# A two-layer Perceiver kernel: in the mixer's loop, the products with X one tile ahead of the next tile's B and C products, and each tile's norm one iteration later

## The chip, the core and the metric

The kernel runs on one core of a Trainium2 chip, in one launch. The metric is the device time of the launch in microseconds (us). Each engine of the core works through its own queue of instructions in order and waits on semaphores for the others: TensorE (PE: matrix products and transposes), VectorE (DVE: elementwise work and reductions), ScalarE (ACT: functions from a loaded table, and copies), GpSimd (POOL: elementwise work) and SyncE (SP: here it only issues DMAs).

## What is computed

Sixteen sequences of 64 tokens with 512 features pass through two layers, each of a cross attention, a mixer or self attention, and a feed-forward part, always as `x = x + f(layernorm(x))`. The change lies in the first layer's mixer, and what comes right behind it is the feed-forward part with a router:

```
x = x + _L0_attn_ref(_layernorm(x), ...)     # the mixer
x = x + _L0_ffn_ref(_layernorm(x), ...)      # 16 blocks, a router keeps 4 of them for each token

# mixer, for each of 16 heads
logA = einsum('hoc,bthc->btho', W_logA, x) + b_logA
XBC  = silu(einsum('hoc,bthc->btho', W_XBC, x) + b_XBC)      # X: 32, B: 64, C: 64 channels
cum  = cumsum(logA over t);  diff = cum[i] - cum[j]
A_ss = where(causal, exp(diff), 0)
G    = einsum('bihn,bjhn->bhij', C, B)
Y    = einsum('bhij,bjhc->bihc', A_ss * G, X)
gate = einsum('hoc,bthc->btho', W_gate, x) + b_gate
out  = (gate * Y).reshape(B, T, D) @ W_out.T + b_out
```

## The kernel before

The 1024 tokens lie as G = 8 tiles of 128 tokens (two sequences each). A tile's residual is `x[:, g, :]`, and `xnT` holds the normed tokens transposed, features on partitions, as the products want them. All data is 32-bit float, and every matrix product shows up as two records in the profile.

A norm is four steps: `ln_stats` (L114, two DVE instructions), `ln_scale` (L118, a square root on ACT and a reciprocal on DVE), `ln_norm` (L122, one DVE instruction that makes `xn`), and `ln_transpose` (L128, four PE transposes and an ACT copy into `xnT`). `ln_out` (L137) is the last two. ACT has one table of functions at a time. Square root, exponential and Silu are in different ones, and copies are in all of them, so each change from one to another costs a table load, which stands in ACT's queue.

The mixer is the stage at L527 to L673. First come the X channels and log A of all tiles (`make_x`), the gates (`make_gate`) and, for tiles 0 to 3, the B and C channels (`make_bc`: sixteen products into eight wide PSUM buffers, each emptied by two Silus). Then the loop over g has for each tile:

- `front(g)`: POOL makes `rt` (L608), PE sums it over time into `pd` (L612, two products), and ACT takes its exponential `ea` (L622). PE makes `pg`, the 32 products of B and C (L619). DVE masks `pg` into `mt` (L624) and multiplies `mt` by `ea` (L625).
- `back(g)`: PE makes `py`, the 32 products of X and `mt` (L637). DVE multiplies the gate by it (`gT`, L640). PE projects with `wout` (L643, four products), DVE adds that to `x` (L644).

The loop emits `front(g)` and then `back(g - 1)` and `ln_stats(g - 1)`. The square roots of tiles 0 to 3 are taken together at g == 4, those of 4 to 6 behind the loop. `ln_out` follows from g == 5 on with tiles 0 to 2, and tiles 3 to 6 behind the loop. At g == 4, `make_bc(1)` makes B and C of tiles 4 to 7. The last tile's `ln_out` stands in the feed-forward stage (L780).

What order the engines see isn't this one. The stage isn't pinned (only stage 1 uses `keep_in_program_order`), so a scheduler reorders each engine's queue when the kernel is built. In the built kernel before, PE's period is: `py(g-1)`, `pd(g+1)`, one product of `pg(g+1)`, the projection of g-1, [a transpose], the other 31 products of `pg(g+1)`.

PSUM is tight: `pw2` (L557) has three wide buffers of two banks for `pd`, `pg`, `py` and `pbc` in turn, and `ps2` (L556) two of one bank. `tmp` (L555) has two buffers of each of `rt`, `ea`, `mt`.

Behind the mixer stands the feed-forward stage (L686 on). Its `route(q)` (L721) needs `rwz`, a padded copy of the router's weights, which POOL makes (L702) from a DMA (L689). The route is a PE product `pr`, an ACT copy `lp`, PE's `pl`, seven DVE steps up to `rank`, and PE's transposes `pt` (L748). Its masks go to DRAM and come back by DMA (L750, L757), and DVE multiplies the hidden values by them (L773). In between, pieces of the last layer's weights are brought to their grid (`piece_load`, `piece_scale`, `piece_round`, `piece_store`, L156 to L176): a DMA in, three small DVE steps, one on POOL (L167), one on DVE (L171), one on POOL (L175), and a DMA out. Two of those pieces come right behind the mixer, in SBUF that `mt` used.

## Time and profile before

| | us |
|---|---|
| median of 3 runs | 2061.74 (2059.08 to 2063.44) |
| the profiled execution's own time | 2065.08 |
| its span, from first to last instruction | 2063.4 |
| PE busy in the span | 1957.7 (95%) |
| DVE, ACT, POOL busy | 1216.9, 804.8, 622.3 |
| mixer, from its first product to the router's first (1190.85 to 1299.26) | 108.4 |
| its loop, from the first `pg` (1216.95) to there | 82.3 |
| PE busy from 1217.0 to 1299.3 (19.96 + 18.20 + 22.87 + 11.15 in four stretches) | 72.2 |
| PE busy from 1312.0 to 1460.0 (32.91 + 55.00 + 60.00 in three stretches) | 147.9 of 148.0 |

The times of instructions count from the span's start. A row of the timeline is a run of equal instructions: start, duration, engine, line, operation, tile written and tiles read, shape, number of records, and in brackets how long the engine had been idle before it and what ended that. PE starts the next product before the last one's result is out, so work on PE is best measured from start to start[...]. The clock granted to PE was full in all stretches from 1190 to 1460.

### The profile page before, as it was taken

The numbers are of one execution on the slowest core, as the hardware profiler recorded it, in microseconds if no ns is written. First come the engines' busy times: TensorE is split into PE (matmuls) and PEld (weight loads), VectorE is DVE, ScalarE is ACT, GpSimd is POOL, SyncE is SP. The second block draws the span as 40 slices with busy tenths as digits, with TensorE's granted clock in tenths as the row PEclk, the third lists the DMA queues.
The fourth block names the chain that finished last, engine by engine and source line by source line (L and its number), as shares of the span: only waits on it lengthen the run. The fifth ranks groups of instructions, "written<-read, shape, count | busy, mean of one in ns | idle before, by whom it ended". The sixth has DMA issues, their size and how long they took to land. (4 is left out here: it accounts for less than half of the span.)

```text
span 2063.4 us, 39030 instructions
## 1 busy us (share of the span) xinstructions
PE 1957.7 (95%) x17197; PEld 1236.0 (60%) x17197; DVE 1216.9 (59%) x1869; ACT 804.8 (39%) x1112; POOL 622.3 (30%) x463
## 2 busy tenths in 40 slices
PE   8999999999999999999999798899998999999779
PEld 4677777777777677777777654444453455444334
DVE  2577777777777777777777654711113334429751
ACT  2445454545454544545454443201102123317700
POOL 0346454445445454635454321300003000000100
PEclk9999999999999999999999899999999999999889
DMA  5011101101110111011100120510236971200001
GB/s 207 22 54 44 45 20 54 44 24 42 51 46 17 48 44 54 12 54 44 54 12 17 32 103 22 197 50 31 84 131 247 347 278 62 71 0 10 21 0 41
DMA packets 61754, 141.13 MB, mean 68 GB/s; under 512 B 4448, under 2 KB 31600, under 8 KB 60432
## 3 DMA queue, kind: packets, MB, share of 16 engines
q1 hardware_dynamic: 61584, 138.63, 18.9%
q8 instruction: 135, 2.21, 0.5%
q14 instruction: 35, 0.29, 0.1%
HBM read 127.02 MB, written 11.60 MB: 67 GB/s over the span
## 5 line engine op out<-in xcount | busy, mean ns | idle before, releaser
L204 PE MATMUL ps<-wkv,ctxT 128*128 128x256 f32 (+1 forms) x1664 | 399.7, 388 | 16.5 <-DVE vt L229 16.3
L204 PE MATMUL ps<-ctxT,wkv 128*128 128x400 f32 (+1 forms) x1024 | 365.6, 503 | 12.7 <-DMA ctxT<-in_ctxT_dram 8.8
L204 PEld LDWEIGHTS ps<-wkv,ctxT 128*128 128x128 f32 (+1 forms) x1664 | 295.9, 185 | 96.2 <-DVE vt L229 26.8
L338 POOL TENSOR_TENSOR acc<-acc,st 128x1024 f32<-128x1024 f32 x124 | 319.6, 2577 | 23.0 <-ACT st L331 17.9
L265 ACT COPY st<-sc 128x1024 f32<-128x1024 f32 x192 | 191.7, 1016 | 320.5 <-PE sc L204 284.3
L229 DVE TENSOR_TENSOR vt<-ps,rows 128x256 f32<-128x256 f32 (+1 forms) x416 | 170.7, 421 | 202.0 <-PE ps L204 201.8
L204 PEld LDWEIGHTS ps<-ctxT,wkv 128*128 128x128 f32 x1024 | 189.7, 191 | 141.3 <-issue 12.8
L323 DVE TENSOR_TENSOR st<-st,nb 128x1024 f32<-128x1024 f32 (+1 forms) x224 | 239.1, 1139 | 34.3 <-PE nb L317 34.3
L218 ACT ACTIVATE kt<-ps,cols 128x400 f32<-128x400 f32 (+1 forms) x256 | 152.3, 595 | 271.2 <-PE ps L204 271.2
L331 ACT ACTIVATE st<-st 128x1024 f32<-128x1024 f32 (+1 forms) x224 | 212.1, 992 | 7.3 <-DVE st L323 6.9
L204 PEld LDWEIGHTS sc<-qd,kt 64*128 64x128 f32 x3072 | 179.2, 188 | 36.5 <-issue 24.2
L204 PE MATMUL sc<-qd,kt 64*128 64x128 f32 x3072 | 197.8, 278 | 1.6 <-ACT st L265 1.6
L336 POOL TENSOR_TENSOR acc<-st 128x1024 f32<-128x1024 f32 x31 | 73.0, 2356 | 353.3 <-issue 221.2
L280 DVE TENSOR_TENSOR rm<-rm,sc 128x512 f32<-128x512 f32 x256 | 168.5, 679 | 10.7 <-PE sc L204 3.8
L204 PE MATMUL av<-st,vt 128*32 128x64 f32 x6656 | 108.7, 223 | 8.8 <-DVE xnT L365 8.8
L59 PE MATMUL ps<-xnT,w 128*128 128x512 f32 x256 | 112.2, 594 | 0.0
L59 PE MATMUL ps<-w,hT 128*128 128x512 f32 x256 | 110.2, 592 | 0.0
L204 PEld LDWEIGHTS av<-st,vt 128*32 128x32 f32 x6656 | 98.5, 112 | 18.1 <-ACT st L331 9.1
L167 POOL TENSOR_TENSOR w<-w,winv 128x512 f32<-128x512 f32 x36 | 37.9, 1055 | 192.3 <-DVE winv L166 181.7
L59 PE MATMUL po<-wdT,gate 128*128 128x512 f32 x192 | 85.2, 607 | 3.2 <-DVE gate L1231 3.2
L1209 POOL TENSOR_TENSOR gate<-up,gate 128x1024 f32<-128x1024 f32 x4 | 9.5, 2385 | 259.0 <-ACT up L1208 259.0
L59 PEld LDWEIGHTS ps<-w,hT 128*128 128x128 f32 x256 | 48.6, 190 | 61.2 <-issue 61.2
(236 smaller groups left out, 2249.6 us busy)
## 6 DMA issues: line engine op xcount, KB each, us to landing
cT<-in_ctxT_dram SPq DMA_DIRECT2D x16, 1601.0 KB, 10.6
cN<-in_ctx_dram SPq DMA_DIRECT2D x16, 1536.0 KB, 9.7
ctxT<-in_ctxT_dram SPq DMA_DIRECT2D x15, 1601.0 KB, 7.3
grid<-w SPq DMA_DIRECT2D x36, 256.0 KB, 2.0
w<-grid SPq DMA_DIRECT2D x36, 256.0 KB, 2.7
w<-in_w_dram SPq DMA_DIRECT2D x2, 4096.0 KB
mk<-kept SPq DMA_DIRECT2D x16, 512.0 KB, 3.9
w<-in_wgate_dram SPq DMA_DIRECT2D x12, 256.0 KB, 2.6
```

The costliest lines, as they stand in the source:

```text
L59: pe.matmul(out, lhsT=lhsT, rhs=rhs, start=start, stop=stop)
L167: pin(gp.tensor_tensor(w, w, inv.unsqueeze(2).to_broadcast([P, 16, 32]), ALU.mult))
L204: pin(pe.matmul(out, lhsT=lhsT, rhs=rhs, start=start, stop=stop))
L218: pin(s.activation(kts[u, i][:, o:o + n], ps[:, :n], AF.Identity, bias=col(C_BK0 + c)))
L229: pin(v.tensor_tensor(t[:n, :], ps[:n, :], row(R_BV0 + e, 256)[:n, :], ALU.add))
L265: pin(s.copy(st[:, ks[0]:ks[-1] + 1, r * 256:(r + 1) * 256], sc[r]))
L280: pin(v.tensor_tensor(rm, rm, sc[r][:, z:z + 2, :], ALU.max))
L323: pin(v.tensor_tensor(f[:m, k:k + n, :], f[:m, k:k + n, :], nb[:m].unsqueeze(1).to_broadcast([m, n, 512]), ALU.add))
L331: pin(s.activation(f[:m, k:k + n, :], f[:m, k:k + n, :], AF.Exp))
L336: pin(gp.tensor_tensor(accs[u], f[:, 0:2, :], f[:, 2:4, :], ALU.add))
L338: pin(gp.tensor_tensor(accs[u], accs[u], f[:, k:k + 2, :], ALU.add))
L1209: gp.tensor_tensor(gate[:, f, :], up[:, f, :], gate[:, f, :], ALU.mult)
```

## The change

`front` is split into `decay(g)` (`rt` and `pd`) and `mixing(g, pd)` (`pg`, `ea`, `mt`), and `back` into `gated(g)` (`py`, `gT`) and `mixed(g)` (projection, addition to `x`, and now the norm's statistics, square root and reciprocal of this one tile). The loop emits `decay(g)`, `gated(g-1)`, `mixing(g)`, `mixed(g-1)`, `ln_out(g-2)`.

```
-            lah = la[:, g, :].rearrange("p (m r) -> p r m", r=2).unsqueeze(3).to_broadcast(shape)
...
-            return g, mt
-        def back(g, mt):
+            return mt
+        def gated(g, mt):
...
             v.tensor_tensor(gv, gv, pv, ALU.mult)
+        def mixed(g):
             po = ps2.tile([P, 512], F32, name="ps", tag="mm")
             for c in range(4):
                 mm(po, gT[:, c, g * P:(g + 1) * P], wout[:, c, :], c == 0, c == 3)
             v.tensor_tensor(x[:, g, :], x[:, g, :], po, ALU.add)
+            ln_stats(g)
+            ln_scale(g, g + 1)
...
-        pending = None
+        mt = None
         for g in range(G):
             if g == 4:
                 make_bc(1)
-            new = front(g)
-            if pending is not None:
-                back(*pending)
-                ln_stats(g - 1)
-                if g == 4:
-                    ln_scale(0, 4)
-                if g >= 5:
-                    ln_out(g - 5, ps2)
-            pending = new
-        ln_scale(4, 7)
-        back(*pending)
-        ln_stats(G - 1)
-        ln_scale(G - 1, G)
-        for g in range(3, G - 1):
-            ln_out(g, ps2)
+            pd = decay(g)
+            if g:
+                gated(g - 1, mt)
+            mt = mixing(g, pd)
+            if g:
+                mixed(g - 1)
+            if g >= 2:
+                ln_out(g - 2, ps2)
+        gated(G - 1, mt)
+        ln_out(G - 2, ps2)
+        mixed(G - 1)
```

What the scheduler makes of it, read from the built kernels, is this. No product, elementwise step or DMA is added or taken away except for the square roots and what belongs to them: eight square roots with eight reciprocals in place of three and three, and fifteen table loads in place of six from the first `ea` to the router.

- **PE** up to `pg(0)`: as before. Then in each iteration: `pd(g)`, `py(g-1)`, `pg(g)` in one piece, projection of g-1, transposes of g-2. The sixteen products of `make_bc(1)` stand in one piece behind the transposes of tile 1. The end is: ..., projection of 6, transposes of 5, `py(7)`, transposes of 6, projection of 7, three products of the feed-forward part, the router's `pr`. Before, it was `py(7)`, projection of 7, transposes of 3, 4, 5, 6, `pr`. Between `pr` and the transposes `pt` stand 9 products of the feed-forward part as before, so with the three ahead 12 are done by `pt`.
- **ACT** in each iteration: `ea(g)`, copy of the transposed tile g-2, table load, square root of g-1, table load, `ea(g+1)`.
- **DVE** in each iteration: both steps of `mt(g)`, addition to `x` of g-1, statistics of g-1, reciprocal, `xn` of g-1, `gT(g)`.
- **POOL**: the `rt` are as before, and the additions of the next bias to `x` (L143), each behind its tile's `xn`, stand between them; they stood behind all `rt`. Behind the mixer, both steps of both pieces now stand ahead of the making of `rwz`.
- **SP** behind the mixer: two piece loads, the store of the first piece, the load of the router's weights, the load of `w2` (4 MB). Before, the router's weights and `w2` stood ahead of that store.

More of the change, by code (lines that the diff above doesn't have):

```diff
@@ L599, in make_bc, with decay @@
                         s.activation(t_[:, pair, :], ps[:, r, :], AF.Silu, bias=col(b_ + pair))
-        def front(g):
-            BT, CT = bcs[g // 4]
-            shape = [P, 2, 8, LQ]
-            upto4 = upto.unsqueeze(1).unsqueeze(1).to_broadcast(shape)
+        shape = [P, 2, 8, LQ]
+        upto4 = upto.unsqueeze(1).unsqueeze(1).to_broadcast(shape)
+        def decay(g):
             lah = la[:, g, :].rearrange("p (m r) -> p r m", r=2).unsqueeze(3).to_broadcast(shape)
@@ L612, in front, with mixing @@
                 mm(pd[:, r, :], later, rt[:, r].rearrange("p m i -> p (m i)"))
+            return pd
+        def mixing(g, pd):
+            BT, CT = bcs[g // 4]
             pg = wide("pg")
```

## The prediction

> **What bounds the kernel now.** I read the page first: PE is busy for 1957.7 of 2063.4 us, so only time that PE loses can be won, and an edit that doesn't change PE's work is worth what it changes in PE's waits. Then I took the table of stretches. PE is busy for 147.9 of the 148.0 us from 1312.0 to 1460.0, behind the mixer, but for only 72.2 of the 82.3 us of the mixer's loop (front table). The list of PE's waits between 1210 and 1345 says for what:

> ```profile
> PE ps L59 <- DVE gT L640: 4.4, 7, 1.1
> PE py L59 <- DVE mt L625: 2.2, 1, 2.2
> PE pt L748 <- DVE rank L745: 2.0, 1, 2.0
> PE ps L131 <- DVE mv L116: 1.3, 1, 1.3
> PE ps L131 <- DVE xn L124: 0.9, 1, 0.9
> PE pd L59 <- ACT ea L622: 0.8, 1, 0.8
> PE ps L131 <- DVE x L644: 0.4, 1, 0.4
> ```

> These are 12.0 us in all: the projection waits for the gate in each iteration, the rest is at the loop's end and in the router. This is all that a new order can win. PE's timeline shows one period:

> ```profile
> 1267.33 3.70 PE L59 MATMUL ps<-wout,gT 128*128 128x512 f32 x8 [0.65 <-DVE gT L640]
> 1270.87 0.60 PE L131 MATMUL ps<-ident,xn 128*128 128x128 f32 x4
> 1271.39 1.16 PE L59 MATMUL pg<-CT,BT 64*64 64x64 f32 x62
> 1272.48 0.86 PE L59 MATMUL py<-mt,X 64*32 64x64 f32 x64
> 1273.27 1.98 PE L59 MATMUL pd<-rt,later 128*128 128x512 f32 x4
> 1275.18 0.32 PE L59 MATMUL pg<-CT,BT 64*64 64x64 f32 x2
> 1276.12 3.70 PE L59 MATMUL ps<-wout,gT 128*128 128x512 f32 x8 [0.62 <-DVE gT L640]
> ```

> From start to start: projection 3.54, transposes 0.52, pg 1.09, py 0.79, pd 1.91. That is 7.85 of work in a period of 8.79, so some 0.9 is lost in each.

> **The change, one period worked out.** S is the start of the projection of g-2. Without waits PE runs transposes at S+3.54, pd(g) at 4.06, py(g-1) at 5.97, pg(g) at 6.76, the next projection at 7.85. py no longer waits (mt(g-1) was ready a projection ago), and pg now lies between py and the projection as cover for gT (0.68). But gT has a new neighbour ahead of it in DVE's queue: the norm of g-2 with its own square root. That chain, with durations of the same timelines: projection's result S+3.70, x 0.72, statistics 0.73 and 0.18, so mv at S+5.37. ACT meanwhile copies the transposes (done S+4.82) and then loads the square root's table:

> ```profile
> 1266.51 1.28 ACT L622 ACT_TABLE_LOAD   x1 [1.87 <-PE pd L59]
> 1267.80 1.02 ACT L622 ACTIVATE ea<-pd 128x1024 f32<-128x1024 f32 x1
> ```

> 1.29 from load to next instruction: square root at S+6.12 to 6.42, reciprocal, xn from 6.66 to 7.2, gT to 7.9. The projection starts at S+7.9. So a period costs 7.9, with 0.05 of wait in place of 0.9. The second load (to the exponential) ends at S+7.7, ea(g) at 8.7, and mt's second step asks for it at 9.3: hidden, with 0.6 to spare.

> **Against it, first: the tables.** [...] The row shows no gap around the load, and I take it.

> **Against it, second: POOL.** rt(g+2) starts when pd(g) is out, S+6.04, and runs 1.91. What DVE's xn does beside POOL shows here (timeline, both engines, at the loop's end):

> ```profile
> 1294.97 1.04 POOL L167 TENSOR_TENSOR w<-w,winv 128x512 f32<-128x512 f32 x1
> 1295.12 1.56 DVE L124 TENSOR_SCALAR xn<-x,mv,rstd 128x512 f32<-128x512 f32 x1
> ...
> 1297.01 1.26 POOL L143 TENSOR_TENSOR x<-x,rows 128x512 f32<-128x512 f32 x1
> 1297.20 1.36 DVE L124 TENSOR_SCALAR xn<-x,mv,rstd 128x512 f32<-128x512 f32 x1
> ```

> xn takes 0.54 by itself, but 1.56 and 1.36 where it starts behind a POOL instruction: it sits until POOL is through. In the new period xn comes at S+6.66, half a us behind rt, so it is held to S+8.0, gT ends at 9.25, and the projection starts at S+9.2: 1.35 lost, more than before. That hits the iterations in which both stand together, xn of tiles 1 and 3 with rt of tiles 5 and 7 (xn of 0 has slack, xn of 2 falls into the B and C products, and from tile 4 on no rt is left). Bounds: 0 if xn gets in first, 2.7 for both. I take 2.7.

> **The loop's sum**, as starts of projections, from pg(0) at 1216.95, which nothing ahead moves. Tile 0: pd(1) and then py(0) waits 0.8 for the first mt: 1222.65. Tile 1 (no transposes): +7.37, 1230.0. Tile 2: +7.85 +1.35, 1239.2. Tile 3: the B and C products lie between. The first Silu comes at about 1246.9 (transposes, copy, two loads, one square root), each buffer is emptied in 1.14 (rows of L599), pd(4) may start when the sixth is, 1253.9, and pd, py, pg follow: 1257.7 (before: 1258.94, with one pd more behind it). Tiles 4, 5, 6: +9.2, +7.9, +7.9, 1282.8. At the end transposes of 5 and py(7) lead to 1287.7, and then the transposes of tile 6 stand ahead of the projection of 7 and need xn of 6, at S+7.2 = 1290.0: 2.4 of wait. Projection of 7 at 1290.5 (before: 1290.71), done at 1294.1. Before, four transposes and 2.6 of waits followed until the router at 1299.26; now they are behind us. So PE is 5.2 ahead.

> **What is given back behind it.** In SP's queue the load of the router's weights now stands behind the store of the first weight piece. That piece may be loaded when py(7) is done: 1287.75, landing 2.7 later (DMA issues) 1290.4. DVE's three steps (0.69, 0.17 held by POOL's L143, 0.24) end at 1292.3. POOL's two L167 take 1.05 each, 1294.45; DVE's L171 is held to there and both end at 1295.3; L175 1.05, 1296.35. Store issued, weights' load at 1296.8, landing 1299.5. POOL copies (L702, 0.44): rwz at 1300.0. PE does three products of the feed-forward part (2.6) to 1296.7 and then waits 3.3 for rwz. The router's pr starts at 1300.0 against 1299.26, but with 2.6 of work done ahead: 1.8 gained. Bounds of this wait: 2.3 to 4.3, by one POOL instruction's length either way.

> The wait for rank (2.0) goes: from pr to pt there are 9 products as before, but DVE is through with its norms, so lg comes right behind pl at 1302.9 (before 1304.0, and 0.8 of its steps lost to POOL) and rank at 1309.5, ahead of PE's 1310.15. The second router starts at 1314.0, before 1318.12: 4.1. There a new wait may come: rank of the second half goes between mask multiplies, the masks come by DMA 1.6 + 5.0 behind their store at 1311.7, so 1318.3 (before 1319.4), then DVE needs 9.6 to rank, 1327.9, and PE is there at 1327.1. 0.8 is given back: the second pt at 1328.1 against 1331.53, **3.4 us gained**. From there PE is dense in before, each mask multiply waiting for ACT and not for a mask, so I carry the gain to the end unchanged. w2 is issued 2.7 later (1297.2), takes some 12 (before: from 1294.5 until the DMA share falls off at 1306), and PE wants it at about 1358 (before 1362.0): hidden. The third piece load behind it, and the kept masks' store at 1311.7, come after w2 has drained.

> The profiled execution takes 2065.08, its span 2063.4; 3.4 less is 2061.7 and 2060.0. The median of the runs is 2061.74: **2058.3 us**.

> **Rivals.** (a) As worked out, 2056.5 to 2060: 0.45. (b) xn and rt don't collide, or the piece chain is shorter, so that rwz is early: 2.7 of collisions and 3.3 of wait are open, 6.0 in all; half of it gives 2055.3, all of it 2052.3. For it: the collision hangs on half a us; against it: xn waits for a table load that can't start before the copy. 0.25. (c) The gain moves into the router: the masks' store falls behind w2's 4 MB, which fills the queues for 12 us; each us of that delays the second rank and pt by one, and with 2 to 3 us nothing is left: 2061. The times say that w2 is drained at 1309; 0.2. (d) Slower: the switch of tables costs more than the row says, on the chain square root, xn, gT. [...] Against it: the rows. 0.1.

> **The numbers.** A measurement of this kernel tells 0.2%, 4.1 us, from no change: below 2057.6 is faster, above 2065.9 slower. (a) lies across the lower border, a quarter to a third of it below (0.13); (b) is below; (c) is no change; (d) is mostly above, with 0.02 of (c). Faster 0.38, same 0.52, slower 0.10. The range leaves out (d) and the far end of (b): 2054.5 to 2062.5.

> **What would show it.** Projections (L59 ps<-wout,gT) 7.9 apart without a wait for gT, but 9.2 for tiles 2 and 4, with xn of 1.3 or more in front; a load and the next ACT instruction 1.29 apart; PE's transposes of tile 6 waiting some 2.4 for xn; pr waiting some 3.3 for POOL's rwz; the second pt near 1328. If PE waits for gT in every period, (d) holds; if pr doesn't wait, (b).

## The result, and the profile after

The changed kernel takes 2055.54 us (median of 17 runs, 2050.64 to 2061.67), the kernel before 2062.47 (17 runs, 2059.08 to 2068.25); the ratio is 0.9965, 95% interval 0.9955 to 0.9974. That is some 7 us less (5.4 to 9.3 by the interval), where 3.4 were predicted. The profiled execution took 2056.32, its span 2054.6 (before 2065.08 and 2063.4).

A difference of two single spans says little here. In the fourteen profiles of this study, repeats of both kernels among them, the first `pg` of the loop starts anywhere between 1214.3 and 1217.5, though next to nothing ahead of it was touched. So I count from the first `pg`, and to the first product with `w2` (PE L59 ps<-w,hT), by which all of the router is over: 145.06 us before (1216.95 to 1362.01), 139.96 after (1215.15 to 1355.11). **5.1 us come from there.** The list of PE's waits, of 1210 to 1345 as before (line, what is waited for: us in total, times, longest):

```profile
PE ps L131 <- DVE xn L124: 2.3, 1, 2.3
PE ps L59 <- DVE gT L645: 2.2, 2, 1.1
PE pbc L59 <- ACT BT L599: 2.1, 1, 2.1
PE py L59 <- DVE mt L630: 0.8, 1, 0.8
PE pr L59 <- POOL rwz L709: 0.8, 1, 0.8
```

8.2 us in place of 12.0, and quite other ones: seven waits for gT have become two, those for rank and for the last mt are gone, and there is a new one of 2.1 in the B and C products, where ACT stands at a square root before its Silus. The list gives 3.8 of the 5.1. The rest is hidden in PE's busy time (132.85 before, 131.51 after, though the change runs 6.8 us of it at half clock, see below): a period before lost 0.94 from start to start where the list shows 0.65, since the profile's ends of products are modelled.

One period, PE's timeline, without the lines between (transposes, pd, py):

```profile
1265.14 3.70 PE L59 MATMUL ps<-wout,gT 128*128 128x512 f32 x8 [1.11 <-DVE gT L645]
...
1271.72 1.16 PE L59 MATMUL pg<-CT,BT 64*64 64x64 f32 x64
```

The next projection starts at 1272.94, 7.80 later: pg in one piece covers gT. The first line is one of the two that were predicted to wait. Why it does is seen in the other one, tile 2's (first DVE, then POOL, then ACT, timelines of the same stretch):

```profile
1234.77 1.60 DVE L124 TENSOR_SCALAR xn<-x,mv,rstd 128x512 f32<-128x512 f32 x1
...
1234.17 1.91 POOL L608 TENSOR_TENSOR rt<-upto,la 128x1024 f32<-128x1024 f32 x1 [4.13 <-PE pd L59]
...
1232.94 1.28 ACT L119 ACT_TABLE_LOAD   x1
1234.24 0.29 ACT L119 ACTIVATE rstd<-mv,eps 128x1 f32<-128x1 f32 x1
```

xn starts 0.6 behind rt and ends only when rt is through: 1.60 in place of 0.55. And a table load is followed by its instruction after 1.30.

The loop's end:

```profile
1287.94 0.68 PE L131 MATMUL ps<-ident,xn 128*128 128x128 f32 x4 [2.28 <-DVE xn L124]
1288.43 5.29 PE L59 MATMUL ps<-wout,gT 128*128 128x512 f32 x8
1293.57 2.74 PE L59 MATMUL ps<-xnT,w 128*128 128x512 f32 x6
1297.08 1.07 PE L59 MATMUL pr<-xnT,rwz 128*32 128x512 f32 x8 [0.77 <-POOL rwz L709]
```

The projection of tile 7 takes 5.14 to the next product, not 3.54. This is the clock. In the table of stretches (us, busy time and count of PE, PEld, DVE, ACT, POOL, then the granted clock, DMA share, GB/s) it is at half speed here, and it was so once more, in the B and C products:

```profile
1288.00:1290.00 2.00, 2.00 (x6) 1.09 (x7) 1.58 (x5) 0.58 (x1) 1.24 (x1) 0.61 0.24 93
1290.00:1292.00 2.00, 2.00 (x4) 0.84 (x3) 0.99 (x4) 0.00 (x0) 1.74 (x2) 0.53 0.03 8
```

Both falls of the clock come behind waits of PE of over 2 us. The kernel before had a wait of 2.2 and one of 2.0 and kept its clock; the last section has what differed.

### The profile page after: what moved, and what is told of

Read it like the earlier page. It is cut to its first block, busy times and chain, and to the rows that moved or that the text cites. A ratio compares the mean times of both kernels' runs of the same rounds, so it can differ in the third digit from the quotient of the medians.

```text
span 2054.6 us, 39042 instructions
## 1 busy us (share of the span) xinstructions
PE 1953.4 (95%) x17197; PEld 1234.5 (60%) x17197; DVE 1214.8 (59%) x1874; ACT 817.1 (40%) x1126; POOL 621.4 (30%) x463
## 5 line engine op out<-in xcount | busy, mean ns | idle before, releaser
L59 PE MATMUL ps<-xnT,w 128*128 128x512 f32 x256 | 112.4, 594 | 0.0
L59 PE MATMUL ps<-w,hT 128*128 128x512 f32 x256 | 110.2, 592 | 0.0
L167 POOL TENSOR_TENSOR w<-w,winv 128x512 f32<-128x512 f32 x36 | 38.3, 1064 | 195.0 <-DVE winv L166 180.2
L59 PE MATMUL po<-wdT,gate 128*128 128x512 f32 x192 | 85.5, 609 | 3.2 <-DVE gate L1238 3.2
L59 PEld LDWEIGHTS ps<-w,hT 128*128 128x128 f32 x256 | 48.6, 190 | 61.2 <-issue 61.2
```

The costliest lines, as they stand in the source:

```text
L59: pe.matmul(out, lhsT=lhsT, rhs=rhs, start=start, stop=stop)
L167: pin(gp.tensor_tensor(w, w, inv.unsqueeze(2).to_broadcast([P, 16, 32]), ALU.mult))
```

## The experiments

Theory 1: the order of the products makes the gain (pg as cover for gT), and the norms in the loop take a part of it back. Theory 2: the norms do it, since four transposes and their waits no longer stand between the loop and the router. All runs in one table: the ratio to before, and from the profile the time from the first `pg` to the second router's `pt` and to the first product with `w2`.

| kernel | ratio (95%) | to 2nd pt | to w2 |
|---|---|---|---|
| before; again (2060.89 in one execution) | 1 | 114.58; 114.63 | 145.06; 145.11 |
| changed | 0.9965 (0.9955 to 0.9974) | 109.48 | 139.96 |
| changed, second run | 0.9973 (0.9959 to 0.9987) | 112.18 | 142.66 |
| changed, third (2053.99 in one execution) | | 109.26 | 139.74 |
| order alone | 0.9957 (0.9942 to 0.9971) | 104.88 | 135.36 |
| norms alone | 1.0013 (1.0003 to 1.0023) | 115.15 | 144.77 |
| order, roots in the loop | 0.9967 (0.9954 to 0.998) | 107.08 | 137.56 |
| changed, third rt buffer | 0.9976 (0.9966 to 0.9986) | 107.48 | 137.96 |
| changed, rwz early | 0.9958 (0.9941 to 0.9975) | 109.39 | 139.01 |
| changed, projection 7 ahead | 0.9971 (0.9958 to 0.9985) | 108.99 | 138.61 |
| both of these | 0.9962 (0.9948 to 0.9977) | 108.23 | 137.85 |
| order, rwz early | 0.9935 (0.9919 to 0.9951) | 104.46 | 134.94 |
| the same, transposes of 3 in the gap | 0.9944 (0.9929 to 0.996) | 102.55 | 133.03 |

The last column is one execution and holds what the clock did in it; the ratio holds what the clock did in the rest of the 2050 us.

**The order alone.**

```
         mixed(g):   ln_stats(g)
-                    ln_scale(g, g + 1)
         loop:
-            if g >= 2:
-                ln_out(g - 2, ps2)
+            if g == 4:
+                ln_scale(0, 4)
+            if g >= 5:
+                ln_out(g - 5, ps2)
+        ln_scale(4, 7)
         gated(G - 1, mt)
-        ln_out(G - 2, ps2)
         mixed(G - 1)
+        ln_scale(G - 1, G)
+        for g in range(3, G - 1):
+            ln_out(g, ps2)
```

> Only the order of the products is the changed kernel's (pd(g), py(g-1), pg(g), projection of g-1); the norms stand where the kernel before has them, with square roots taken together for tiles 0-3, 4-6 and 7, and transposes of tiles 3 to 6 behind the loop. Theory 1 (the cover by pg makes the gain): no projection in the loop waits for gT, periods 7.3 to 7.9, the projection of tile 7 some 5 to 7 us earlier behind pg(0) than before's 73.8, the waits for xn and mv at the end (2.6 before) and for rank (2.0) still there; kernel 4 to 6 us faster than before (ratio 0.997 to 0.998). Theory 2 (the norms moved into the loop make the gain): within 1.5 us of before.

8.9 us faster than before, and 9.7 by the first product with `w2`. Projections are 7.23 apart, with transposes 7.67, and none in the loop waits for gT. PE's longest waits (the others are 0.8 for the first mt, 0.4 for x, 0.3 for xn):

```profile
PE ps L59 <- DVE gT L645: 1.1, 1, 1.1
PE ps L131 <- DVE mv L116: 1.0, 1, 1.0
...
PE pr L59 <- POOL rwz L713: 0.8, 1, 0.8
```

The only wait for gT is the last tile's, which has no pg behind it. The wait for rank, expected to stay, is gone too. Theory 1 holds, and its gain (4 to 6) was set too low.

**The norms alone.**

```
         before's loop:
                 back(*pending)
                 ln_stats(g - 1)
-                if g == 4:
-                    ln_scale(0, 4)
-                if g >= 5:
-                    ln_out(g - 5, ps2)
+                ln_scale(g - 1, g)
+            if g >= 2:
+                ln_out(g - 2, ps2)
```

(and behind the loop `back`, the transposes of tile 6, the norm of 7.)

> Only the norms are the changed kernel's (each tile's square root in the loop, transposes one iteration later); the products stand in before's order, with the projection behind pd and one product of pg. Theory 1: every projection still waits about 1.1 or more for gT, some periods are longer by the norm's chain on DVE and ACT, and what is won is only the end: rank's 2.0 and a part of the 2.6; 1 to 3 us faster than before. Theory 2: 5 to 7 us faster, as the whole change.

Slower than before, by some 2 us, so theory 2 falls, and theory 1 had expected 1 to 3 us of gain. PE's waits for gT went down (3.0 in six), but

```profile
PE pbc L59 <- ACT CT L599: 2.7, 1, 2.7
PE py L59 <- DVE mt L625: 1.9, 1, 1.9
```

the B and C products wait for ACT, which takes a square root between two of its Silus, the wait for the last mt stays, and the router waits 1.5 for rwz. By `w2` 0.3 is won, which is nothing; the 2 us that the runs lose (0.6 to 4.7 by the interval) are not in this stretch of its profile. The clock can account for them: each run comes with its granted share, on the mean 0.9841 in these 12 runs and 0.9861 in the 29 of before, and that 0.002 of 2060 us is up to 4. The transposes of three tiles fewer between loop and router are no gain, since they stand in the loop instead (tile 6's still stand behind the last projection here).

**Roots in the loop.** The order alone, with `ln_scale(g, g + 1)` in `mixed` and no joint square roots: all of the change's table loads, but transposes where the order alone has them.

> The order of products alone, and each tile's square root and reciprocal in the loop as in the changed kernel, so with all its table loads; but the transposes stand where the order alone has them (tiles 0 to 2 in iterations 5 to 7, 3 to 6 behind the loop). PE's order is that of the order alone. Theory 1 (what the norms take back comes from xn and the transposes standing in the loop: rt holding xn and so gT, transposes in front of the B and C products and of the last projection; a table switch costs only its load, off PE's path but for the B and C products): projections 7.2 to 7.7 apart without a wait for gT, the B and C products delayed by 1.5 to 2, in all 1 to 2.5 us slower than the order alone (2054 to 2055.5). Rival (the table switches make most of the cost): 4 us or more slower than the order alone, as slow as the changed kernel or slower.

By the profile 2.2 slower than the order alone (137.56 against 135.36), as theory 1 expected; in the run 2055.16 against 2052.92, with intervals that overlap. Both profiles have one stretch of half clock, at pr. PE's waits show where the 2.2 are:

```profile
PE pbc L59 <- ACT BT L599: 1.9, 1, 1.9
```

In the loop there is only this new one; at tile 7's gT PE waits 1.4, 0.3 more than with the order alone. ACT's timeline has the reason:

```profile
1240.55 0.29 ACT L119 ACTIVATE rstd<-mv,eps 128x1 f32<-128x1 f32 x1 [3.29 <-DVE mv L116]
...
1242.15 1.26 ACT L599 ACTIVATE BT<-pbc,cols 128x512 f32<-128x512 f32 x2
```

The square root of tile 2 stands ahead of the first Silu and waits for mv. The Silu comes 27.25 behind the first pg, where it comes at 25.05 with the order alone. In all other periods the loads cost PE nothing. Of the 4.6 between the order alone and the first profile of the change, the roots are 2.2; what is left, 2.4, goes to xn, the transposes in the loop and the clock together, which no run separates. That the norms take something back is seen in the runs only as a tendency: 2052.92 for the order alone against 2056.21 for the change measured beside it, and, with the weights early in both (below), 2050.12 against 2054.58; in each pair the intervals overlap.

**A third buffer for rt** (`bufs=3` at L607).

> The changed kernel with a third buffer for rt, so that POOL makes rt one iteration earlier: rt of tile 7 then runs beside pd(4) and no longer just ahead of xn of tile 3, while rt of tile 6 still falls on xn of tile 1. Theory 1 (the two long periods come from DVE's xn held by POOL's rt): the projection of tile 4 follows that of tile 3 by 7.8 in place of 8.8, its wait for gT of 1.1 is gone, that of tile 2 stays; 1.0 us won by the second router, unless the wait for rwz takes it back. Rival (they come from the square root and its tables): both periods stay at 8.8, no change.

The projections of tiles 3 and 4 in PE's timeline:

```profile
1258.03 3.70 PE L59 MATMUL ps<-wout,gT 128*128 128x512 f32 x8
...
1265.82 3.70 PE L59 MATMUL ps<-wout,gT 128*128 128x512 f32 x8
```

7.79 from projection to projection and no wait, xn 0.55, with the same square root and loads as in the changed kernel: it was rt. Tile 2's wait of 1.11 stayed, as expected. By `w2` this run is 2.0 ahead of the first profile of the change, 0.65 of it because its clock stayed full in the B and C products; its run time doesn't show that (0.9976).

**The router's weights early**: `rw` loaded and `rwz` made in the stage before the mixer.

> The changed kernel with the router's weights loaded and rwz made in the stage before the mixer, so that neither stands behind the weight pieces in SP's and POOL's queues. The router's first pr then comes ahead of the transposes of tile 6. Theory 1 (behind the loop the piece chain on SP and POOL bounds pr, and pr's 1.1 can fill a part of the 2.3 that PE waits for xn): the wait for rwz is gone, that for xn is about 1.2, 1.5 to 3 us faster than the changed kernel (2053 to 2055). Rival (PE's wait for xn of tile 6 and the clock that falls behind it bound the end, and rwz only fills a gap that is there anyway): less than 0.8 us.

The wait for rwz is gone and that for xn is 1.3, but the kernel isn't measurably faster (0.9958, intervals overlap) and by `w2` only 0.95 ahead, though its clock stayed full at the loop's end. PE now waits 1.0 at pl and 0.9 at each pt, because DVE is not ready. Theory 1 (1.5 to 3 us) was too high here, and the rival (under 0.8) comes nearer.

**The projection of tile 7 ahead of the transposes of tile 6**, without and with the early weights:

```
         gated(G - 1, mt)
-        ln_out(G - 2, ps2)
         mixed(G - 1)
+        ln_out(G - 2, ps2)
```

> The changed kernel with the projection of tile 7 ahead of the transposes of tile 6, the router's weights as in the changed kernel. Theory 1: the wait for xn of tile 6 (2.3) is replaced by one of 1.1 for gT, and pr then waits for rwz some 1 to 2; rwz itself comes earlier, since the load of the router's weights is no longer behind the store of the first piece; pr at 79.5 to 80.5 behind pg(0) in place of 81.3 to 81.9, 1 to 2 us faster than the changed kernel. Rival: rwz comes when it came, and nothing is won.

> As the kernel with the early router weights, and the projection of tile 7 ahead of the transposes of tile 6. Theory 1: no wait for xn of tile 6 nor for rwz; in their place some 1.1 for gT of tile 7 between py and its projection; 2 to 4 us faster than the changed kernel (2052 to 2054.5). On the clock: if it falls because PE has stood for 2 us and more, then it holds full speed from 1280 to 1310, since no such wait is left there. Rival: PE's order at the end makes no difference to the early router weights alone.

Without: gT 1.1 and rwz 1.6 in place of xn 2.3 and rwz, pr at 79.05, 1.35 ahead by `w2`; the run (2057.76 in the median, from 2052.4 to 2060.9) doesn't tell it from the changed kernel. With both: 2.1 ahead by `w2`, again not seen in the run, and PE's clock is full from 1280 to 1310 (1.00 in each stretch of 2 us). What pr wins is lost at rank (wait of 1.9). DVE's first and third step there, and POOL beside the first:

```profile
1294.13 2.06 DVE L747 TENSOR_TENSOR gt<-lg 128x1024 f32<-128x1024 f32 x1
...
1298.51 1.23 DVE L749 TENSOR_TENSOR eq<-eq,before 128x1024 f32<-128x1024 f32 x1
...
1292.72 2.39 POOL L175 TENSOR_TENSOR w<-w,wsc 128x512 f32<-128x512 f32 x2
```

A step takes 1.23 alone, and 2.06 and 2.29 (the second step, which runs beside POOL's L143) beside POOL. The earlier router runs into the pieces' steps, which it came behind before.

**The order with early weights**, and the same with the transposes of tile 3 between the last py and the last projection:

> The order of products alone (norms as in the kernel before) with the early router weights. Theory 1 (the order makes the gain, the norms in the loop take about half of it back): 0.8 to 2 us faster than the order alone, so 9 to 11 us faster than before (ratio about 0.995). Rival (the measured gain of the order alone is helped by chance in the clock): 5 to 7 us faster than before.

> As the order alone with early router weights, and the transposes of tile 3 between the last py and the last projection, the square roots of 4 to 6 behind them. Theory 1: 0.5 of the 1.1 wait for gT of tile 7 is filled, the chain of mv, square root and xn of tile 7 is unchanged; 0.5 to 1 us faster than without this, 10 to 12 us faster than before. Rival: xn of tile 3 stands ahead of gT in DVE's queue beside POOL's work on the pieces, held by it for 1 us, and nothing is won.

The first is the fastest kernel measured: 2050.12, some 12 us faster than before, where the order alone had 8.9 (the intervals overlap). Its longest waits:

```profile
PE pt L760 <- DVE rank L757: 2.4, 2, 1.2
PE ps L59 <- DVE gT L651: 1.1, 1, 1.1
```

The first pr comes 2.75 earlier than in the order alone and the pl behind it 2.85, of which 1.65 is half clock that the order alone had between pr and pl; two waits for rank then give most back: 0.4 by `w2`. The rest of the 2.8 in the run is more likely the clock, which in this profile keeps full speed from 1200 to 1920 in every stretch of 20 us. The second is 1.9 ahead by `w2`, with gT's last wait down to 0.6, and not faster in the run (2051.63). The runs don't separate the two.

**Both kernels again, for the clock.**

> The changed kernel once more, unchanged, to see what repeats: if PE's halved clock behind the waits of 2.1 and 2.3 us (two stretches of some 3 us in its loop) is a consequence of the waits, it is there again at the same places; if it is chance, it lies elsewhere or nowhere, and pr then waits about 2.3 to 2.6 for rwz in place of 0.8.

> The kernel before once more, for its clock and its waits. If PE's clock falls behind many but not all of the waits of 2 us and more, then it may fall here behind py's wait for mt (2.2) or pt's for rank (2.0), which it did not in the first profile; by 1.7 us for each stretch at half clock. If it never falls here, waits for other things count.

> The changed kernel a third time, for its clock: the two waits of 2.1 (B and C products) and 2.3 (xn of tile 6) should be there again, with half clock behind at least one of them, and the wait for rwz 0.8 if the clock falls behind the second and 2.1 if it doesn't.

Before, again: same waits to a tenth, no half clock between 1190 and 1360. The third run of the change is like the first. The second has no half clock behind the wait for xn, so pr waits 2.1 for rwz, and behind that the clock falls for longer:

```profile
1300.00:1302.00 2.00, 2.00 (x8) 1.43 (x7) 0.00 (x0) 0.69 (x1) 0.00 (x0) 0.50 1.22 524
...
1304.00:1306.00 2.00, 2.00 (x4) 0.76 (x3) 1.90 (x3) 0.00 (x0) 0.00 (x0) 0.55 1.06 459
```

From pr to pt it took 13.47 for the 10.16 of the first profile: 3.3 lost, with nothing to hide them. Hence 112.18 for 109.48 with the same program.

## Why the prediction was right, and where its sizes were off

The measured time, 2055.54, lies in the range of 2054.5 to 2062.5; 2058.3 was predicted. It is below the 2056.5 at which rival (a), the sum as worked out, ends, beside the 2055.3 that (b) gives for half of its terms, and under the border of 2057.6 for faster, which got 0.38. The mechanism in the loop was as forecast, with rwz somewhat early, as (b) has it. The gain by the second pt was 5.1, 2.4 and 5.3 in the three profiles, for the 3.4 of the sum. Some of the agreement is luck: two terms of the sum cost less than it had, and the clock, for which it has no term, cost more, by a different amount in each profile. Times from the first pg, predicted and in the three profiles of the change:

| | predicted | first | second | third |
|---|---|---|---|---|
| projection of tile 2 | 22.25 | 21.87 | 21.87 | 21.87 |
| of tile 3 | 40.75 | 41.15 | 40.90 | 41.14 |
| of tile 4 | 49.95 | 49.99 | 49.75 | 49.99 |
| of tile 7 | 73.55 | 73.28 | 73.04 | 73.28 |
| feed-forward | 77.15 | 78.42 | 76.47 | 78.41 |
| pr | 83.05 | 81.93 | 81.31 | 81.70 |
| second pr | 97.05 | 96.05 | 98.75 | 95.83 |
| second pt | 111.15 | 109.48 | 112.18 | 109.26 |

- **The period (7.9)**: 7.80, where PE's own work takes 7.67 (the order alone). So gT sets it, as the working has it.
- **xn held by rt for tiles 1 and 3**: right in place, 1.1 each and not 1.35; the third rt buffer took one of them away. By the rows xn took 1.60 both times, from 0.6 behind rt's start to 0.3 behind its end, and 0.55 without rt beside it.
- **The table switches**: load to next instruction 1.30, as the row said (1.29). Rival (d) falls. No run shows a cost of a switch beyond its load, so nothing measured puts (d) above the border of 2065.9, as the chances have it: by the roots in the loop, all loads together cost 2.2, almost all in one place, the B and C products, which the sum had in it (a first Silu 29.95 behind the first pg; it came at 29.55).
- **The wait for rwz (3.3)**: mis-sized. It measured 0.8, 2.1 and 0.6. Without half clock ahead of it, PE stands there for 2.1, a little below the lower bound of 2.3. The chain from the end of py(7) to rwz took 11.4 (1285.67 to 1297.03), predicted 12.25: the load of the weights was issued 0.5 sooner behind py(7), it landed in 2.5 and not 2.7, and the copy took 0.24 for 0.44.
- **The 0.8 given back at the second pt**: not there. rank was ready at 1324.48 and PE at 1324.63. The first mask multiply came 6.95 behind the masks' store (6.6 predicted), but the store came 1.3 sooner behind the first pg than the sum had it, and from that multiply to rank it took 8.9 and not 9.6; the first of the ranking's large steps ran ahead of it. In the first and third profile pr came 1.1 and 1.35 sooner than the sum had it, and with the 0.8 that is about the 1.7 and 1.9 by which their second pt beat it.
- **The clock**: not foreseen. In the B and C products it took some 0.4 to 0.65 in all three (tile 3's projection comes at 40.50 in the two related kernels, third rt buffer and projection 7 ahead, that kept their clock there). In the first and third profile it took 1.6 from the projection of tile 7, hidden for the most part by the wait for rwz, in the second 3.3 behind pr, hidden by nothing.
- **Where the gain is from**: the prediction names pg as cover, which is right, but lists the end ("now they are behind us") as another gain of the change. It isn't a gain of the norms: by the profiles the order alone wins 9.7 by `w2`, and with the norms in the loop as well 5.1 are left.

What stays open: by `w2` the gain was 5.1 to 5.4 in two profiles and 2.4 in one, against about 7 in the first set of runs (5.4 to 9.3 by the interval) and 5.6 in the second (2.7 to 8.5). Behind the first product with `w2` the profiles of these kernels need 694 to 705 us for the same work. Most of that spread is the clock: each profile has 31 to 49 us at half clock there, and with half of that taken off, 676 to 681 are left (679.1 and 679.2 before, 677.7 to 678.6 for the change). So some 1 us may have been won there too, but it is no more than the spread among the other kernels.

## What to carry over

Put work that waits for nothing between a product and the next one that needs its result, and keep the queue of the engine in between clear. A norm with a square root moved into such a loop isn't free because PE has gaps: its cost appears where ACT stands at the root in front of something urgent (2.2 here) and where DVE meets POOL (1.1 a time). When a change makes one engine earlier, ask what it then runs beside: the earlier router lost its gain to POOL's pieces. And on PE, count the waits that can fall into one stretch of 3.4 us together, not the longest one alone: from 1214 to 1480 half clock came behind all 12 stretches in which PE stood for 0.52 or more.

## What the hardware did that was not expected

**Half clock behind waits of 2.1 us.** Of the waits of PE of 2.0 to 2.7 us between 1215 and 1320, over all profiles, the clock fell behind the B and C products in six of eight, behind that for xn in three of four, behind the one for rwz of 2.1 in its one case, and behind none of the four of the kernel before. One fall lasts some 3.4 us at half speed (the shares of 0.61 and 0.53 in the two stretches of 2 us shown above come to 1.72 lost, so 3.44 at half), once double that. It also fell in two kernels behind a row of waits of 0.3 to 1.4 that add up to some 3.6 within 10 us (the order alone and the roots in the loop, at pr).

| profile, and what PE waited for | stretch | share in which PE stood | clock behind it |
|---|---|---|---|
| before, the last mt (2.2) | 1279.89 to 1283.31 | 0.34 | full |
| | 1283.31 to 1286.72 | 0.34 | full |
| changed, xn (2.3) | 1285.03 to 1288.45 | 0.67 | half |
| changed, second run, xn (2.3) | 1285.30 to 1288.71 | 0.50 | full |
| changed, second run, rwz (2.1) | 1295.54 to 1298.95 | 0.62 | half |
| order alone, a row of short waits | 1285.97 to 1289.38 | 0.60 | half |

So a wait of 2.1 that fell into one stretch (0.62) had half clock behind it, waits of 2.2 and 2.3 cut in two by the grid (0.34 and 0.34; 0.50) had not, and short waits that added up to 0.60 within one stretch had. Where the grid lies differs from run to run, as the table's stretches show: a border at 1288.45 in the first profile of the change, at 1288.71 in the second. From 30 to 2040 us this is nearly as sharp: half clock came behind all 45 stretches in which PE stood for over 0.57, behind 22 of 43 between 0.46 and 0.57, and behind 6 of 7906 below that, all six between 1526 and 1543, where PE's records show no pause; these stay unexplained, and so does why the fall at 1299.0 lasted two steps.
